# A layer of a graph network on one core: destinations' rows from a table in memory, 28 of 48 copied columns on VectorE, a ring of twenty groups

## The chip, the core and the metric

The kernel runs on one core of a Trainium2 chip. The core has five engines with a queue of instructions each: TensorE (PE in the profile; PEld is its loading of weights), VectorE (DVE), ScalarE (ACT), GpSimd (POOL) and SyncE (SP, which issues DMAs). An engine's queue is worked off in order by its sequencer; the profile writes what the sequencer does itself, such as loading registers, with a q behind the engine's name (DVEq), and does not count it as busy time. The metric is the time on the device, in microseconds.

## What is computed

One message-passing layer with a residual and a layer norm. There are 12500 nodes with 64 features and 212500 edges, sorted by destination, with 32 features each.

```python
msg_in = jnp.concatenate([nodes[row], nodes[col], edge_features], axis=-1)
messages = relu(msg_in @ mW1 + mb1) @ mW2 + mb2
aggregated = jax.ops.segment_sum(messages, col, num_segments=nodes.shape[0])
upd_in = jnp.concatenate([nodes, aggregated], axis=-1)
x = layernorm(nodes + relu(upd_in @ uW1 + ub1) @ uW2 + ub2)
```

`row` is the source of an edge and `col` its destination. All is in 32-bit floating point.

## The kernel before

The edges are cut into 554 groups of 384, a group into three tiles of 128 edges. Since the edges are sorted by destination, the destinations of one group lie in a window of 32 consecutive nodes, whose first node is known from the list `firsts`. One step of the main loop (`for k in range(G)`, line 560) works on several groups at once, each in a different stage:

- `gather` (line 146): GpSimd fetches the source nodes' 64 features of a group, one indirect DMA for each tile of 128 rows, into a ring of buffers `own_s`. The ring has `RING = AHEAD + 4 = 8` groups. A gather that fills a buffer anew waits for the transpose of the group that had it before.
- `onehot` (line 326): VectorE compares each edge's destination with the 32 positions of the window and writes a matrix of zeros and ones beside the gathered features.
- `turn(k)` (line 335): TensorE transposes the three tiles, features and one-hot columns together; ScalarE copies the result into `own_st`, where the edges' own features already lie.
- `hidden(k - 2)` (line 361): TensorE multiplies `own_st` by the matrix `own_wm` of the group. Its first 64 rows are the source's part of `mW1`, its last 32 the edge's part; the 32 rows in the middle hold, for each node of the window, that node's features times the destination's part of `mW1` (the window's rows). There are `NW = 8` such matrices, used in turn. ScalarE then applies the relu (`own_h`).
- `sums(k - 4)` (line 387): TensorE sums the hidden rows by destination with the one-hot matrix and counts the edges; VectorE adds both to `agg` and to a row of `own_xc`, at the window's place (lines 406 and 407).

The window's rows come about in two parts. `places` (line 296), every fourth step, loads the first nodes of four windows into VectorE's registers and copies the four windows out of `own_xc`, the transposed features of all nodes, which lie in SBUF. `windows` (line 311) multiplies the four by the destination's part of `mW1` in one product on TensorE; VectorE copies the result into four of the matrices `own_wm` (line 320).

Not every tile is gathered. The first tile of some groups is put together column by column: `fetch` (line 475) loads the addresses of some source nodes into registers (line 490) and copies one column of `own_xc` into `own_st` for each edge (lines 503 and 505). From step `BEGIN = 18` to step 543 there are 40 columns a step: VectorE takes batches of 8 and 12, ScalarE batches of 12 and 8. Each batch is one register load of as many registers, and then as many copies of 64 partitions by 4 bytes. The groups so served are listed in `COPIED`. The addresses come by SyncE's queue for eight steps at a time (`indexes`), and VectorE turns them into byte addresses (`addresses`).

Twenty-five blocks of 512 nodes are finished as soon as no later edge can reach them (`update`, line 413), one part a step: the second products, the statistics, the normalisation, and the output by SyncE's queue. The last `SHORT = 10` groups go through the stages one after the other, so that the end is short.

The order of work is the order in which the program writes it, engine by engine (`manual_schedule`). In one step VectorE's queue holds the two additions, in every fourth step the four copies of line 320, the comparison, then a register load, 8 columns, a register load, 12 columns, and in every fourth step the load and copies of `places`. `step` (line 524) puts all of a step's products behind one wait, and what follows them waits for the last product of the step.

Of the kernel before, what the change touches and what calls it, by code (L numbers as in the profile page):

```python
# [10 lines left out]
F32 = mybir.dt.float32  # L11
# [23 lines left out]
AHEAD = 4  # L35
# [9 lines left out]
NEAR_GROUPS = 24  # L45
# [4 lines left out]
VCOLS = (8, 12)  # L50
# [29 lines left out]
PLAN = plan()  # L80
COPIED = []
# [27 lines left out]
def ordered(ctx: ExitStack, tc: tile.TileContext, a, own, ok):  # L109
# [6 lines left out]
    xwp = ctx.enter_context(tc.tile_pool(name="xw", bufs=2))  # L116
# [29 lines left out]
    def gather(g):  # L146
# [9 lines left out]
        for i in loads[g]:  # L156
            after(i, *([turn_by[g // 2 * 2 + 1 - RING]] if g >= RING else []))
# [55 lines left out]
    nc.vector.memset(high[:, :NEAR_GROUPS], float(NEAR_NODES - W))  # L213
# [33 lines left out]
    starts, xws, indices, columns_by = {}, {}, {}, {}  # L247
# [48 lines left out]
    def places(b):  # L296
# [8 lines left out]
        xw = xwp.tile([D + 2, SB, W], F32, name="xw")  # L305
        for i in range(n):
            starts[g + i] = v[i]
            nc.vector.tensor_copy(xw[:, i, :], xc[:, bass.ds(v[i], W)])  # L308
        xws[b] = xw, n

    def windows(b, wp, own_bank=True):


        xw, n = xws.pop(b)
        did = nc.tensor.matmul(wp[: n * W, :], xw[:, :n, :], w1b, start=True, stop=True)  # L315

        def copies():
            for i in range(n):
                g = b * SB + i
                c = nc.vector.tensor_copy(wm[g % NW][D : D + W, :], wp[i * W : (i + 1) * W, :])  # L320
                after(c, *([did] if own_bank else []), *([hidden_by[g - NW]] if g >= NW else []))
                wm_by[g] = c

        return did, copies
# [62 lines left out]
    def sums(g, ps):  # L387
# [14 lines left out]
        def add(step):  # L402
            sums_by[g] = step
            at = bass.ds(starts.pop(g), W)
            return [
                after(nc.vector.tensor_tensor(agg[:, at], sg[:, 0, :], agg[:, at], ALU.add), step),  # L406
                after(nc.vector.tensor_tensor(xc[D : D + 1, at], counted,  # L407
                                              xc[D : D + 1, at], ALU.add), step),
            ]
# [65 lines left out]
    def fetch(k):  # L475
# [4 lines left out]
        if n == 0:  # L480
            indexes(i + 1)
        if n == SPAN - 2:
            addresses(i + 1)
        c0 = (k - BEGIN) * COLS
        for engine, count in [*((ET.DVE, c) for c in VCOLS), *((ET.Activation, c) for c in ACOLS)]:
# [21 lines left out]
            c0 += count  # L507
# [16 lines left out]
    def step(*work):  # L524
# [9 lines left out]
        copies = None  # L534
        for part, g, *_ in parts:
# [389 lines left out]
```

## Time and profile before

| | |
|---|---|
| median of 3 runs | 1899.2 us (1896.05 to 1899.49) |
| the profiled execution | 1895.48 us |
| its span, first to last instruction | 1893.5 us |
| granted TensorE clock, mean | 0.969 |
| instructions in the span | 58044 |
| gathers on GpSimd | 1497 |
| columns on VectorE, on ScalarE | 10500, 10492 |

A row of a group gives the line, the engine, the operation, what is written and read, and the count; behind the bar the busy time in us and the mean of one in ns; behind the second bar the idle time of the engine just before, and what ended most of it. "issue" means that the engine waited for nothing that the profile shows as a wait. A row of the order in time gives start and length in us, and the idle time in brackets. A row of one line's instructions gives the shortest, the median and the longest duration in ns, and the first and the last start in us.

### The profile page before, as it was taken

The numbers are of one execution on the slowest core, as the hardware profiler recorded it, in microseconds if no ns is written. First come the engines' busy times: TensorE is split into PE (matmuls) and PEld (weight loads), VectorE is DVE, ScalarE is ACT, GpSimd is POOL, SyncE is SP. The second block draws the span as 40 slices with busy tenths as digits, with TensorE's granted clock in tenths as the row PEclk, the third lists the DMA queues.
The fourth block names the chain that finished last, engine by engine and source line by source line (L and its number), as shares of the span: only waits on it lengthen the run. The fifth ranks groups of instructions, "written<-read, shape, count | busy, mean of one in ns | idle before, by whom it ended". The sixth has DMA issues, their size and how long they took to land. (4 is left out here: it accounts for less than half of the span.)

```text
span 1893.5 us, 58044 instructions
## 1 busy us (share of the span) xinstructions
PE 1361.4 (72%) x12209; PEld 1193.4 (63%) x12209; DVE 1492.9 (79%) x13761; ACT 1550.7 (82%) x11818; POOL 1417.6 (75%) x1504
## 2 busy tenths in 40 slices
PE   3776777677777777677676776877767767767777
PEld 3666666666666666666665666666666656666665
DVE  3578888778888788887888878878888887888873
ACT  3489889888888888988988888889888888898882
POOL 7777777777777777777777777777777777777774
PEclk9999999999999999999999999999999999999999
DMA  6322222222222222222222222222222222222221
GB/s 136 73 46 45 46 48 44 50 43 48 46 45 48 47 43 50 45 46 44 48 50 43 48 46 45 46 48 44 50 44 47 47 48 44 47 44 50 44 47 29
DMA packets 68440, 92.50 MB, mean 49 GB/s; under 512 B 30893, under 2 KB 38350, under 8 KB 68078
## 3 DMA queue, kind: packets, MB, share of 16 engines
q0 software_dynamic: 47904, 49.12, 14.7%
q1 hardware_dynamic: 19260, 39.12, 7.4%
q14 instruction: 260, 2.13, 0.4%
q8 instruction: 102, 1.67, 0.4%
q10 hardware_dynamic: 914, 0.46, 0.1%
HBM read 85.29 MB, written 3.20 MB: 47 GB/s over the span
## 5 line engine op out<-in xcount | busy, mean ns | idle before, releaser
L149 POOL DMA_INDIRECT own_s<-in_x,src_sb x1497 | 1416.8, 946 | 457.3 <-issue 407.5
L503 DVE COPY own_st<-own_xc 64x4 uint8 x10500 | 897.7, 190 | 231.0 <-issue 217.9
L505 ACT ACTIVATE own_st<-own_xc 64x4 uint8 x10492 | 1057.1, 194 | 18.2 <-issue 15.2
L341 PE MATMUL own_ps<-own_ident,own_s 128*96 128x128 f32 x1661 | 289.5, 285 | 496.0 <-DMA own_s<-in_x,src_sb 157.9
L341 PEld LDWEIGHTS own_ps<-own_ident,own_s 128*96 128x96 f32 x1661 | 169.3, 132 | 566.1 <-ACT own_h L377 240.7
L394 PE MATMUL own_ps<-own_s,own_h 128*128 128x128 f32 x3322 | 480.5, 283 | 4.1 <-ACT own_h L377 2.9
L366 PE MATMUL own_ps<-own_wm,own_st 128*128 128x128 f32 x3322 | 479.4, 283 | 0.0
L351 ACT ACTIVATE own_st<-own_ps 96x384 f32<-96x384 f32 (+2 forms) x718 | 293.2, 408 | 205.8 <-PE own_ps L399 104.7
L394 PEld LDWEIGHTS own_ps<-own_s,own_h 128*128 128x128 f32 x3322 | 432.6, 199 | 6.3 <-ACT own_h L377 4.7
L366 PEld LDWEIGHTS own_ps<-own_wm,own_st 128*128 128x128 f32 x3322 | 432.1, 199 | 1.4 <-issue 0.5
L377 ACT ACTIVATE own_h<-own_ps 128x384 f32<-128x384 f32 x553 | 263.9, 477 | 16.0 <-PE own_ps L366 16.0
L399 PE MATMUL own_ps<-own_s,own_one 128*1 128x32 f32 x3322 | 190.1, 194 | 0.0
L320 DVE COPY own_wm<-own_ps 32x128 f32<-32x128 f32 x550 | 156.9, 285 | 5.6
L399 PEld LDWEIGHTS own_ps<-own_s,own_one 128*1 128x1 f32 x3322 | 114.5, 84 | 69.4 <-issue 6.2
L329 DVE TENSOR_TENSOR own_s<-iota,dlc 128x96 f32<-128x96 f32 x554 | 142.4, 258 | 14.3 <-issue 0.2
L406 DVE TENSOR_TENSOR agg<-own_ps,agg 128x32 f32 x554 | 105.1, 190 | 59.5 <-PE own_ps L399 25.9
L407 DVE TENSOR_TENSOR own_xc<-own_ps,own_xc 1x32 f32 x554 | 101.2, 183 | 30.6 <-PE u_ps L425 11.4
L308 DVE COPY xw<-own_xc 66x32 f32 x554 | 73.0, 207 | 15.5 <-DMA own_xc<-in_xT 9.8
L315 PE MATMUL own_ps<-w1b,xw 66*128 66x128 f32 (+1 forms) x276 | 69.1, 333 | 0.0
L446 ACT ACTIVATE rstd<-mv,eps 128x4 f32<-128x4 f32 (+1 forms) x25 | 7.4, 297 | 55.3 <-DVE mv L444 55.3
L437 PE MATMUL u_ps<-u,u 128*128 128x64 f32 (+1 forms) x196 | 50.1, 399 | 0.5 <-ACT u L427 0.5
L437 PEld LDWEIGHTS u_ps<-u,u 128*128 128x128 f32 (+1 forms) x196 | 47.1, 324 | 2.2 <-ACT u L427 0.9
(62 smaller groups left out, 276.7 us busy)
## 6 DMA issues: line engine op xcount, KB each, us to landing
own_st<-in_efT SPq DMA_DIRECT2D x138, 192.0 KB
own_s<-in_x,src_sb POOLq DMA_INDIRECT x1497
xin<-in_x SPq DMA_DIRECT2D x24, 128.0 KB
out<-o SPq DMA_DIRECT2D x24, 128.0 KB
own_xc<-in_xT SPq DMA_DIRECT2D x12, 179.2 KB
index<-in_src_copied SPq DMA_DIRECT2D x65, 1.2 KB
dlc_i<-in_dst_cols SPq DMA_DIRECT2D x1, 831.0 KB
own_xc<-in_xT SPq DMA_DIRECT2D x4, 179.5 KB
```

What stands on the lines that cost most here:

```text
L149: nc.gpsimd.indirect_dma_start(out=s[:p, j, :D], out_offset=None, in_=x[:, :], in_offset=bass.IndirectOffsetOnAxis(ap=src_sb[:p, g * TG + ...
L320: c = nc.vector.tensor_copy(wm[g % NW][D : D + W, :], wp[i * W : (i + 1) * W, :])
L329: places_by[g] = nc.vector.tensor_tensor(own.s[g % RING][:, :, D:], iota.unsqueeze(1).to_broadcast([P, TG, W]), dlc[:, g * TG : (g + 1) * ...
L341: nc.tensor.transpose(xt[:, j * P : j * P + p], s[:p, j, :], ident[:p, :p])
L351: after(nc.scalar.activation(t[r, c : c + n][:, m], xt[r, m], AF.Copy), step)
L366: nc.tensor.matmul(pre[:p, j, :], t[:, c + j * P : c + j * P + p], wm[g % NW], start=True, stop=True)
L377: relu_by[g] = [nc.scalar.activation(h, pre, AF.Relu)]
L394: did.append(nc.tensor.matmul(sg, h[:p, j, :], s[:p, j, D:].unsqueeze(1).to_broadcast([p, TIMES, W]), start=j == 0, stop=j == len(sizes) - 1))
L399: did.append(nc.tensor.matmul(counted, own.one[:p], s[:p, j, D:], start=j == 0, stop=j == len(sizes) - 1))
L406: after(nc.vector.tensor_tensor(agg[:, at], sg[:, 0, :], agg[:, at], ALU.add), step),
L503: by[engine] = nc.vector.tensor_copy(o, x_at)
L505: by[engine] = nc.scalar.activation(o, x_at, AF.Copy)
```

## The change

Three things change together.

The ring of gathered groups grows from 8 to 20 buffers (`AHEAD` from 4 to 16), and a gather now waits for the transpose of exactly the group that had its buffer.

The window's rows are no longer worked out window by window. A table of all nodes' products with the destination's part of `mW1` is written to memory in 25 blocks of up to 512 nodes: two before the loop, the others in every third step (`projected`: four small products on TensorE, a copy on ScalarE, a DMA by SyncE's queue). For each group SyncE reads 32 rows of the table straight into the matrix `own_wm` (`window`), four steps ahead of the group's transpose; the first node is loaded into SyncE's registers for four groups at a time. VectorE's copies of lines 308 and 320 and TensorE's product of line 315 are gone; VectorE still loads the first nodes for its own additions. Limits on the windows' places (`LIMITS`) see to it that no row is read before its block is written.

Columns grow from 40 to 48 a step: on VectorE batches of 12, 8 and 8, on ScalarE 12 and 8 as before. The three batches on VectorE are no longer together: the first stands between the two additions, the second after them, the third after the comparison.

```diff
-AHEAD = 4
+AHEAD = 16
 RING = AHEAD + 4
-NEAR_GROUPS = 24
+EVERY = 3
+LIMITS = (0, 24, 48)
-VCOLS = (8, 12)
+VCOLS = (12, 8, 8)
 ACOLS = (12, 8)
...
-            after(i, *([turn_by[g // 2 * 2 + 1 - RING]] if g >= RING else []))
+            after(i, *([turn_by[g - RING]] if g >= RING else []))
...
         for i in range(n):
             starts[g + i] = v[i]
-            nc.vector.tensor_copy(xw[:, i, :], xc[:, bass.ds(v[i], W)])
-        xws[b] = xw, n
-
-    def windows(b, wp, own_bank=True):
...
+    def projected(c):
+        base, n = TABLE[c]
+        ps = ups.tile([H, CH], F32, name="u_ps").rearrange("p (n h) -> p n h", n=4)
+        for j in range(n):
+            nc.tensor.matmul(ps[:, j], xc[:, base + j : base + n * P : n], w1b,
+                             start=True, stop=True)
+        t = rowp.tile([P, 4, H], F32, name="t")
+        nc.scalar.activation(t[:, :n], ps[:, :n], AF.Copy)
+        written.append(after(nc.sync.dma_start(
+            by_dst[base : base + n * P, :].rearrange("(p n) h -> p n h", n=n), t[:, :n])))
+
+    def window(g):
...
+        if g % SB == 0:
+            n = min(SB, G - g)
+            _, v = nc.values_load_multi_w_load_instructions(
+                start_i[0:1, g : g + n], engines=[ET.SP], min_val=0, max_val=N - 1,
...
+        wm_by[g] = nc.sync.dma_start(wm[g % NW][D : D + W, :],
+                                     by_dst[bass.ds(rows_at.pop(g), W), :])
+        after(wm_by[g], *written, *([hidden_by[g - NW]] if g >= NW else []))
+        written.clear()
...
-            return [
-                after(nc.vector.tensor_tensor(agg[:, at], sg[:, 0, :], agg[:, at], ALU.add), step),
-                after(nc.vector.tensor_tensor(xc[D : D + 1, at], counted,
-                                              xc[D : D + 1, at], ALU.add), step),
-            ]
+            a = after(nc.vector.tensor_tensor(agg[:, at], sg[:, 0, :], agg[:, at], ALU.add), step)
+            if between:
+                between.pop()()
+            return [a, after(nc.vector.tensor_tensor(xc[D : D + 1, at], counted,
+                                                     xc[D : D + 1, at], ALU.add), step)]
...
-    windows(0, ups.tile([H, CH], F32, name="u_ps")[:, :H], False)[1]()
+    projected(0)
+    projected(1)
+    for g in range(SB):
+        window(g)
...
+        if k % EVERY == 0 and 0 < k // EVERY < len(TABLE) - 1:
+            projected(k // EVERY + 1)
...
         if k < G - SHORT:
+            between.append(lambda: fetch(k, 0))
             step((turn, k), *([(hidden, k - 2)] if k > 1 else []),
                  *([(sums, k - 4)] if k > 3 else []))
             made, summed = max(0, k - 1), max(0, k - 3)
+            if between:
+                between.pop()()
+            fetch(k, 1)
...
+        window(k + SB)
         onehot(k + 2)
-        fetch(k)
+        if k < G - SHORT:
+            fetch(k, *range(2, len(VCOLS + ACOLS)))
```

`fetch(k, *parts)` now emits the batches named by `parts`; the loading of the next addresses and their arithmetic moved to the end of the step.

54 lines of the change are left out of this document (24 added, 30 removed).

## The prediction

> **What bounds the kernel now.** I read the page's busy times first, then the gathers' rows early and late, then VectorE's own order in time, because the change moves work from GpSimd to VectorE.
>
> ```profile
> PE 1361.4 (72%) x12209; PEld 1193.4 (63%) x12209; DVE 1492.9 (79%) x13761; ACT 1550.7 (82%) x11818; POOL 1417.6 (75%) x1504
> L149 POOL DMA_INDIRECT own_s<-in_x,src_sb x1497 | 1416.8, 946 | 457.3 <-issue 407.5
> ```
>
> ScalarE shows the largest share, but GpSimd is the bound: its 1497 gathers take 1416.8 us and the 457.3 us before them are fixed gaps of 0.3 us. The longest wait tells that:
>
> ```profile
> POOL own_s L149 <- issue: 407.5, 1337, 0.3
> L149 POOL DMA_INDIRECT own_s<-in_x,src_sb x59 | 57.1, 968 | 19.1 <-issue 17.1 <-DMA src_sb<-in_src 1.4 <-DMA own_s<-in_x,src_sb 0.3
> L149 POOL DMA_INDIRECT own_s<-in_x,src_sb x1411 | 1334.1, 946 | 430.0 <-issue 383.7 <-DMA own_s<-in_x,src_sb 35.1 <-PE own_ps L399 10.1
> L149 POOL DMA_INDIRECT own_s<-in_x,src_sb x1497: 901/944/1612, 2.9 to 1874.8; - x188
> ```
>
> The second row is the window from 4 to 78 us, before any column is copied, the third from 82 to 1845 us. (1334.1 + 430.0)/1411 = 1.250 us a gather, without a break from 2.9 to 1874.8 us. A step (a group of 384 edges) has 3 - 40/128 = 2.6875 gathers, so 3.36 us; that times 526 steps is the middle of the kernel. The last gather starts 18.7 us before the end of the span of 1893.5 us.
>
> The other limit is close. VectorE's rows, a stretch of its order in time, then its register loads in two windows that hold one load each (eight registers, then twelve; the ScalarE rows are left out):
>
> ```profile
> 80.24 0.19 DVE L406 TENSOR_TENSOR agg<-own_ps,agg 128x32 f32 x1 [4.26 <-PE own_ps L399]
> 80.46 0.18 DVE L407 TENSOR_TENSOR own_xc<-own_ps,own_xc 1x32 f32 x1
> 80.68 0.26 DVE L329 TENSOR_TENSOR own_s<-iota,dlc 128x96 f32<-128x96 f32 x1
> 81.15 0.66 DVE L503 COPY own_st<-own_xc 64x4 uint8 x8 [0.22 <-ACT own_h L377]
> 82.32 0.96 DVE L503 COPY own_st<-own_xc 64x4 uint8 x12 [0.51 <-issue]
> 83.20 0.17 DVE L406 TENSOR_TENSOR agg<-own_ps,agg 128x32 f32 x1
> 83.40 0.18 DVE L407 TENSOR_TENSOR own_xc<-own_ps,own_xc 1x32 f32 x1
> 83.62 0.26 DVE L329 TENSOR_TENSOR own_s<-iota,dlc 128x96 f32<-128x96 f32 x1
> 83.79 0.73 DVE L503 COPY own_st<-own_xc 64x4 uint8 x8
> 84.96 0.95 DVE L503 COPY own_st<-own_xc 64x4 uint8 x12 [0.43 <-issue]
> ```
> ```profile
> L490 DVEq TENSOR_LOAD <-index x1: 594/594/594, 1006.8 to 1006.8; - x1
> L490 DVEq TENSOR_LOAD <-index x1: 844/844/844, 1007.7 to 1007.7; - x1
> L490 DVEq TENSOR_LOAD <-index x1050: 591/843/1118, 80.5 to 1844.6; - x175
> L301 DVEq TENSOR_LOAD <-start_i x139: 340/344/594, 13.8 to 1863.6; - x139
> ```
>
> Before each batch of columns VectorE's queue loads the batch's addresses into registers. The loads don't count as busy, yet the queue does nothing else meanwhile: four registers take 344 ns, eight 594, twelve 844, which is 62.5 ns a register and some 94 ns a load, whatever the engine does. From the first column of a batch of eight to the first of the batch of twelve pass 82.32 - 81.15 = 1.17 us, and 84.96 - 83.79 = 1.17 again: the load's 0.844 and eight columns at 0.04 us of the queue. From 82.32 to 83.79, 1.47 us, it is twelve columns (0.49), the load of eight (0.594), and 0.39 for the two sums, the comparison and their address arithmetic. So one step needs 1.17 + 1.47 = 2.64 us of VectorE's queue, though its columns occupy the engine only (0.95 - 0.66)/4 = 0.072 us each (a batch of twelve against one of eight). Where VectorE catches up with GpSimd, the queue's 2.64 us is its pace, not the engine's.
>
> **The change, part by part.**
>
> Gathers: 1497 become 1465 (48 columns a step make a 128-row tile every 2.67 steps). That is 32 x 1.250 = 40 us less on GpSimd, and 2.625 x 1.250 = 3.28 us a step.
>
> Columns on VectorE: batches 8, 12 become 12, 8, 8, the first between the two sums, the second after them, the third after the comparison. The queue's work by the numbers above: loads 0.844 + 2 x 0.594 = 2.03, columns 28 x 0.04 = 1.14, the rest 0.39, together 3.56 us against 2.64. The instructions beside which the loads now stand are cover for the engine, not for the queue, which has no slack of its own left: 3.56 is over 3.28.
>
> Windows: VectorE loses two copies a step; beside them the rows of what else its queue has:
>
> ```profile
> L320 DVE COPY own_wm<-own_ps 32x128 f32<-32x128 f32 x524 | 149.5, 285 | 5.3
> L308 DVE COPY xw<-own_xc 66x32 f32 x524 | 69.2, 207 | 2.3 <-issue 2.3
> L473 DVE TENSOR_SCALAR index<-index 1x320 int32<-1x320 int32 x64 | 24.0, 374 | 0.0
> L439 DVE TENSOR_TENSOR y<-u_ps,xin 128x256 f32<-128x256 f32 x23 | 9.8, 424 | 18.3 <-PE u_ps L437 18.2
> L443 DVE BATCH_NORM_STATS2 stats<-y 128x6 f32<-128x64 f32 x92 | 18.6, 202 | 0.8
> L444 DVE BATCH_NORM_AGGREGATE mv<-stats 128x2 f32<-128x6 f32 x92 | 16.7, 182 | 3.1
> L454 DVE TENSOR_SCALAR o<-y,mv,rstd 128x64 f32<-128x64 f32 x92 | 23.7, 333 | 0.9
> ```
>
> The two copies are 218.7 us of engine time, 0.42 us a step. In the new kernel that is worth nothing by itself, since the engine (28 x 0.072 + 0.59 from 83.20 to 83.79 = 2.61 us a step) is not what is full; the 2.64 us above held no window. What a step adds beside the 3.56: the load of four starts every fourth step (0.344/4 = 0.09), the index arithmetic every eighth (0.374/8 = 0.05), and one chunk's update every 22 steps (0.42 + 4 x 0.202 + 4 x 0.182 + 4 x 0.333 = 3.3 us, 0.15 a step). The update is engine time and runs partly under the queue's loads: between 0 and 0.15, I take 0.05. Sum: 3.75 us a step, between 3.56 (all three hidden) and 3.85; with the present waits of VectorE for TensorE and ScalarE kept in full, some 0.1 more, 3.95.
>
> SyncE gets 554 window reads and 25 table writes in its queue, and loads of four addresses every fourth step.
>
> ```profile
> L195 SPq DMA_DIRECT2D own_wm<-in_mW x8: 317/582/583, 13.6 to 22.9; - x8
> SPq L289 <- PE own_ps L399: 1113.2, 119, 14.4
> SPq L458 <- DVE own_xc L407: 293.6, 24, 21.8
> ```
>
> A DMA of the window's shape takes SyncE 0.3 to 0.58 us, so under 0.8 us a step with the loads; the queue now waits over 1400 us. A window for group k+4 is sent in step k, after the hidden product of group k-4, and is read in step k+6. Behind it stand only loads two blocks ahead. An output that waits for VectorE holds later windows by a step at most. I cost this at nothing in the middle; the cover is those six steps, over 20 us.
>
> TensorE loses 274 window products and gains 98 small ones, ScalarE gains 25 copies of a bank in the first 72 steps; both wait for others already (ScalarE's 1550.7 us over 554 steps is 2.8 us). Cost nothing.
>
> The ring of 20 groups lets GpSimd run ahead of a slow VectorE. It saves no time where VectorE is the bound.
>
> The start: the first hidden product now waits for the table's first rows.
>
> ```profile
> 13.19 10.66 ACT L243 ACTIVATE agg<-zero 128x12544 f32<-128x12544 f32 x1
> 27.19 1.40 PEld L366 LDWEIGHTS own_ps<-own_wm,own_st 128*128 128x128 f32 x6
> ```
>
> ScalarE is free at 23.9 us, then come two copies, a DMA out and a DMA in. [...]
>
> The end: after step 543 no columns are copied; from 1846 us to the end of the span are 47 us, of which the groups' serial chain (hidden product, relu, sums) is the most and GpSimd little. I take 46.
>
> The sum: 86 + 526 x 3.75 (1972.5) + 46 = 2104.5 us of span, and 2 us around it as in the profiled execution (1895.5 against a span of 1893.5): 2106 us. The median of the runs, 1899.2, lies 0.2% over the profiled execution, and a difference under 0.2% is about what a measurement of this kernel can't tell from no change.
>
> **Rivals.**
>
> 1. The loads are hidden, and GpSimd stays the bound. Then VectorE needs 2.61 us of engine and 0.2 us of updates and index work a step, under 3.28, and the kernel gains the 40 us: 1855. For it: the page puts only 217.9 us of idle on the 1050 loads. Against it: the quickest steps go at the queue's sum. It decides where VectorE's mean step falls below 3.35 us, (1895.5 - 134)/526, that is if 0.4 us of the 3.75 goes under other work (134 as in rival 2).
>
> ```profile
> L503 DVE COPY own_st<-own_xc 64x4 uint8 x10500 | 897.7, 190 | 231.0 <-issue 217.9
> ```
>
> [...]
>
> 2. Each load stalls the engine as now, 217.9 us/1050 = 0.21 us, and no more. Then a step is 2.61 + 3 x 0.21 + 0.2 = 3.44 us and the time 526 x 3.44 + 134 = 1943 (134 is the 86, 46 and 2 of the sum). Against it: the present stall is small because the batch of eight is loaded beside three other operations; with queue and engine nearly in step each load has less to hide under.
>
> 3. The windows come late: TensorE waits for a read behind a waiting output on SyncE's queue. From the product of group g-8, which frees a window's buffer, to that of group g are eight steps, so it decides from 8 x 3.75 = 30 us on. SyncE's two longest waits one behind the other (14.4 and 21.8 us in the rows above) in every round would make it 36.2/8 = 4.5 us a step, 526 x 4.5 + 134 = 2501. Against it: the waits for outputs come 24 times in the whole kernel.
>
> **How the numbers follow.** The queue on VectorE as the bound: 0.79, its own range 2006 (3.56) to 2180 (3.89; the waits of 3.95 in full would be 2212). Rival 2, or a part of the loads hidden: 0.11, 1900 to 2006. Rival 1: 0.08. Rival 3: 0.02. The range from 1950 to 2185 leaves out rivals 1 and 3 and the ends of the others, under 2 in 10. Faster 0.08, same 0.01, slower 0.91.
>
> **What would show it.** Right: VectorE's sums of two successive steps lie 3.5 us apart or more; idle before the columns, put on issue, grows to hundreds of us; GpSimd now waits for TensorE's transposes (its ring is full) and its gathers' gaps exceed 0.3 us; three loads a step of 844, 594, 594 ns; SyncE's window reads land well before use. Wrong: gathers still follow at 1.25 us, or loads that take less, or columns that start during a load.

## The result and the profile after

| | before | after |
|---|---|---|
| median of 4 runs | 1898.1 us | 2262.3 us (2260.3 to 2267.8) |
| ratio, 95% interval | | 1.192 (1.190 to 1.195) |
| the profiled execution, its span | 1895.5, 1893.5 us | 2262.3, 2260.5 us |
| granted TensorE clock, mean | 0.969 | 0.893 |

The direction is the one predicted; the time is 156 us over the predicted 2106 us and 77 us over the end of the range.

The page of the changed kernel, its busy times, the clock by fortieths of the span, and three of its groups:

```profile
PE 1478.4 (65%) x12127; PEld 1309.2 (58%) x12127; DVE 1613.1 (71%) x16799; ACT 1579.4 (70%) x11827; POOL 1384.9 (61%) x1472
...
PEclk9787878899999999899899898898998989999988
...
L153 POOL DMA_INDIRECT own_s<-in_x,src_sb x1465 | 1384.1, 945 | 794.4 <-PE own_ps L416 413.5
L518 DVE COPY own_st<-own_xc 64x4 uint8 x14644 | 1277.9, 185 | 434.5 <-issue 317.1
...
L320 PE MATMUL u_ps<-w1b,own_xc 66*128 66x128 f32 x196 | 53.8, 447 | 104.6 <-DVE own_xc L425 77.6
```

No engine is busy for more than 71% of the span. GpSimd, which TensorE hardly kept waiting before, now idles 794.4 us, more than half of it for TensorE's last product of a step. So its ring is full and something behind it sets the pace. The idle time that VectorE's columns have from "issue", which is where the register loads lie, went from 217.9 to 317.1 us.

VectorE's order in time in the middle of the kernel, one plain step (VectorE's waits are in brackets), and the register loads of the whole kernel:

```profile
999.87 0.17 DVE L422 TENSOR_TENSOR agg<-own_ps,agg 128x32 f32 x1
1000.69 1.12 DVE L518 COPY own_st<-own_xc 64x4 uint8 x12 [0.65 <-issue]
1001.84 0.18 DVE L425 TENSOR_TENSOR own_xc<-own_ps,own_xc 1x32 f32 x1
1002.06 0.66 DVE L518 COPY own_st<-own_xc 64x4 uint8 x8
1002.63 0.24 DVE L346 TENSOR_TENSOR own_s<-iota,dlc 128x96 f32<-128x96 f32 x1
1002.85 0.67 DVE L518 COPY own_st<-own_xc 64x4 uint8 x8
1003.44 0.17 DVE L422 TENSOR_TENSOR agg<-own_ps,agg 128x32 f32 x1
```
```profile
L505 DVEq TENSOR_LOAD <-index x1569: 591/596/866, 98.0 to 2207.3; - x197
```

From sum to sum pass 1003.44 - 999.87 = 3.57 us. The engine is idle for only 0.65 us of them, in front of the batch of twelve; the other two loads stand beside columns that the engine still has to finish. Yet the pace is that of the queue: 3.56 was the prediction's sum of loads, columns and the rest. Measured in the queue, from the start of one load of twelve to the next, the median over the some 284 plain steps from 90 to 530 (no load of four, no index arithmetic, no update) is 3.560 us. From sum to sum the same steps have a median of 3.65 us. All times of plain, statistics and output steps below are from load to load; means over many steps are from sum to sum. Here and below a step bears the number of the group whose sums are added in it, so step 14 is the first one with columns.

Where the time lies, told by two places: the first additions of a step with columns, and the same additions 526 steps later (VectorE's order in time):

```profile
98.03 0.19 DVE L422 TENSOR_TENSOR agg<-own_ps,agg 128x32 f32 x1 [5.03 <-PE own_ps L416]
```
```profile
2213.55 0.19 DVE L422 TENSOR_TENSOR agg<-own_ps,agg 128x32 f32 x1 [0.71 <-PE own_ps L416]
```

| part | predicted | measured | difference |
|---|---|---|---|
| up to the first column batch | 86 | 98.0 | +12 |
| 526 steps at the steady pace | 526 x 3.75 = 1972.5 | 526 x 3.900 = 2051.4 | +79 |
| slower steps at the beginning | 0 | 2115.5 - 2051.4 | +64 |
| the end | 46 | 2260.5 - 2213.55 = 47.0 | +1 |

(2115.5 is 2213.55 - 98.03; 3.900 is the mean from step 134 to step 530.) The four differences are the 156 us. The third row needs a look at the early stage, in which the table is still being written. By twenties from step 14 on the mean step is 5.25, 5.49 and 4.68 us, then 3.77 and 3.90. The three slow twenties lose 74 us, of which some 10 come back: 3 us in the twenty behind them, 8 us in the last ten steps with columns, at 3.12 us each. TensorE and VectorE in this stage (order in time, each engine's waits in brackets):

```profile
149.21 0.34 PE L416 MATMUL own_ps<-own_s,own_one 128*1 128x32 f32 x6
154.49 2.21 PE L320 MATMUL u_ps<-w1b,own_xc 66*128 66x128 f32 x8 [4.95 <-DVE own_xc L425]
156.49 0.85 PE L358 MATMUL own_ps<-own_ident,own_s 128*96 128x128 f32 x3
157.13 1.49 PE L383 MATMUL own_ps<-own_wm,own_st 128*128 128x128 f32 x6
...
162.41 0.83 PE L383 MATMUL own_ps<-own_wm,own_st 128*128 128x128 f32 x6
```
```profile
151.85 0.19 DVE L422 TENSOR_TENSOR agg<-own_ps,agg 128x32 f32 x1
153.16 0.97 DVE L518 COPY own_st<-own_xc 64x4 uint8 x12 [1.12 <-ACT own_st L520]
154.16 0.18 DVE L425 TENSOR_TENSOR own_xc<-own_ps,own_xc 1x32 f32 x1
...
161.42 0.19 DVE L422 TENSOR_TENSOR agg<-own_ps,agg 128x32 f32 x1 [5.13 <-PE u_ps L441]
```

The table's products (line 320) read `own_xc` with all its 66 rows, and one of these rows is the count to which VectorE adds at line 425. The program writes the products behind the additions of the step before, so TensorE has to wait for line 425. TensorE has finished that step's products at 149.55. VectorE, still at the columns of the step before, comes to the first addition only at 151.85, and the second one now stands behind a register load and twelve columns besides: TensorE is idle for 4.95 us, until VectorE has done it at 154.34. Then it is VectorE that waits, 5.13 us, for the step that TensorE begins late. And TensorE is slow behind its pause: six hidden products take 1.49 us instead of 0.83. Windows of the trace show the clock (length; busy time and count of PE, PEld, DVE, ACT, POOL; granted clock, DMA share, GB/s). First the pause and what follows it, then the stage in which the table is written and the rest, all after; last, before, a stretch of the same length from the first columns on:

```profile
149.60:153.40 3.80, 0.00 (x0) 0.00 (x0) 2.33 (x29) 3.21 (x27) 2.83 (x4) 1.00 0.15 28
153.50:160.30 6.80, 5.81 (x30) 5.48 (x30) 2.67 (x28) 0.60 (x1) 5.13 (x6) 0.50 0.35 94
98.00:300.00 202.00, 130.49 (x918) 118.47 (x918) 114.64 (x1202) 117.69 (x869) 124.45 (x133) 0.79 0.22 53
300.00:2208.00 1908.00, 1245.68 (x10474) 1101.20 (x10475) 1457.88 (x15415) 1417.60 (x10885) 1187.51 (x1258) 0.91 0.20 44
```
```profile
81.00:284.00 203.00, 147.85 (x1333) 129.55 (x1332) 161.81 (x1532) 173.45 (x1333) 153.63 (x163) 0.97 0.22 46
```

In 202 us the changed kernel executes 1202 instructions on VectorE where the old one executed 1532, at a granted clock of 0.79 against 0.97. The clock falls while TensorE still stands idle (0.99 from 153.0 to 153.5 us, 0.50 from 153.5 to 154.4, and TensorE starts at 154.49), after the pause the same six products take 1.49/0.83 = 1.8 times as long, and those that start at 162.41 are back at 0.83. In front of the table's products TensorE makes eleven such pauses, of 4.20 to 6.84 us, between 103 and 268 us; the clock is 1.00 in the 2 us ahead of each and 0.50 in the second us behind it. In this stage the clock falls without such a pause too, as the run "Without the row" below shows.

One thing is needed to read the numbers of some experiments: in two sittings the kernel before itself took a third longer (2551.5 and 2559.4 us), and a trace taken there puts hundreds of microseconds on a releaser that the profile doesn't know ("remote"), as in this row from the waits of a kernel with the same loads, columns and products as before; runs of those sittings (called disturbed below) are compared only with each other.

```profile
ACT own_st L351 <- remote: 367.0, 117, 7.7
```

### The profile page after: what moved, and what is told of

Its sections match the earlier page's. It is cut to its first block, busy times and chain, and to the rows that moved or that the text cites. A ratio compares the mean times of both kernels' runs of the same rounds, so it can differ in the third digit from the quotient of the medians.

```text
span 2260.5 us, 63792 instructions
## 1 busy us (share of the span) xinstructions
PE 1478.4 (65%) x12127; PEld 1309.2 (58%) x12127; DVE 1613.1 (71%) x16799; ACT 1579.4 (70%) x11827; POOL 1384.9 (61%) x1472
## 3 DMA queue, kind: packets, MB, share of 16 engines
q8 instruction: 102, 1.67, 0.3%
## 5 line engine op out<-in xcount | busy, mean ns | idle before, releaser
L153 POOL DMA_INDIRECT own_s<-in_x,src_sb x1465 | 1384.1, 945 | 794.4 <-PE own_ps L416 413.5
L518 DVE COPY own_st<-own_xc 64x4 uint8 x14644 | 1277.9, 185 | 434.5 <-issue 317.1
L358 PE MATMUL own_ps<-own_ident,own_s 128*96 128x128 f32 x1661 | 315.3, 304 | 659.7 <-ACT own_h L394 417.9
L411 PE MATMUL own_ps<-own_s,own_h 128*128 128x128 f32 x3322 | 530.9, 303 | 4.2 <-ACT own_h L394 3.6
L383 PE MATMUL own_ps<-own_wm,own_st 128*128 128x128 f32 x3322 | 522.7, 299 | 0.0
L411 PEld LDWEIGHTS own_ps<-own_s,own_h 128*128 128x128 f32 x3322 | 483.1, 219 | 6.4 <-ACT own_h L394 5.2
L383 PEld LDWEIGHTS own_ps<-own_wm,own_st 128*128 128x128 f32 x3322 | 474.8, 215 | 2.2 <-issue 0.5
L320 PE MATMUL u_ps<-w1b,own_xc 66*128 66x128 f32 x196 | 53.8, 447 | 104.6 <-DVE own_xc L425 77.6
L320 PEld LDWEIGHTS u_ps<-w1b,own_xc 66*128 66x128 f32 x196 | 47.5, 327 | 108.3 <-issue 95.6
L323 ACT ACTIVATE t<-u_ps 128x512 f32<-128x512 f32 (+1 forms) x25 | 14.7, 588 | 73.8 <-PE u_ps L320 70.8
```

The source lines that it names most:

```text
L153: nc.gpsimd.indirect_dma_start(out=s[:p, j, :D], out_offset=None, in_=x[:, :], in_offset=bass.IndirectOffsetOnAxis(ap=src_sb[:p, g * TG + ...
L320: nc.tensor.matmul(ps[:, j], xc[:, base + j : base + n * P : n], w1b, start=True, stop=True)
L358: nc.tensor.transpose(xt[:, j * P : j * P + p], s[:p, j, :], ident[:p, :p])
L383: nc.tensor.matmul(pre[:p, j, :], t[:, c + j * P : c + j * P + p], wm[g % NW], start=True, stop=True)
L411: did.append(nc.tensor.matmul(sg, h[:p, j, :], s[:p, j, D:].unsqueeze(1).to_broadcast([p, TIMES, W]), start=j == 0, stop=j == len(sizes) - 1))
L518: by[engine] = nc.vector.tensor_copy(o, x_at)
```

## The experiments

The theory: VectorE's queue sets the pace, through the register loads (0.094 us a load and 0.0625 us a register); besides, the table's products wait for VectorE's addition in the first 74 steps. The rivals: the copies themselves or the table cost the time, the gathers do, or each load costs a fixed stall.

### What the loads are worth

**No loads on VectorE.** The 28 columns are still copied, but from places known when the program is written, so VectorE loads no registers for them.

```diff
-            _, v = nc.values_load_multi_w_load_instructions(
+            if engine == ET.DVE:
+                v = [None] * count
+            else:
+                _, v = nc.values_load_multi_w_load_instructions(
...
-                x_at = xc_bytes[:D, bass.ds(at - own.at, 4)]
+                x_at = (xc_bytes[:D, 4 * c : 4 * c + 4] if at is None
+                        else xc_bytes[:D, bass.ds(at - own.at, 4)])
```

> The changed kernel, but VectorE's 28 columns are copied from fixed places, without register loads (so the copied source features are not the edges' own). If VectorE's queue with its loads is the bound, its step falls from 3.56 us to the engine's 2.6 and the gathers' 3.28 us are the bound: about 1870 us (1855 to 1900). If the copies themselves, the window reads or the chain of products are the bound, it stays above 2150 us.

Measured: 1865.2 us (before 1898.3). Its groups:

```profile
L153 POOL DMA_INDIRECT own_s<-in_x,src_sb x1465 | 1386.0, 946 | 456.4 <-issue 298.3 <-DMA own_s<-in_x,src_sb 109.4 <-PE own_ps L416 43.4
...
L522 DVE COPY own_st<-own_xc 64x4 uint8<-64x4 uint8 x14644 | 1249.8, 186 | 15.7
```

The same 14644 copies of the same 186 ns, without their loads, are 397 us faster, and the gathers are the bound again, (1386.0 + 456.4)/1465 = 1.258 us each. The loads are the price, and neither the engine's part of the copies nor the order of the batches. With the loads the copies' register addresses are gone too; what those cost in the queue this run doesn't separate, but the five loads of four below vary the loads alone. The slow beginning is still there, if shorter (4.27, 4.45 and 3.76 us a step by twenties from step 14), but it costs little in the end: afterwards the steps go at 2.96 to 2.99 us, faster than the gathers' 3.28, until the groups that GpSimd has gathered ahead are used up.

**The change without its eight more columns.**

```diff
-VCOLS = (12, 8, 8)
+VCOLS = (12, 8)
```

> Table and ring as changed, but VectorE's columns back to 20 a step in batches of 12 and 8 (spread as changed). If VectorE's queue is the bound: 3.56 - 0.594 - 8 x 0.04 = 2.65 us and 0.35 of extras a step, under the gathers' 3.36, so 1895 to 1940 us, with some loss left in the first 72 steps. If the table's reads and writes are what is slow, above 2100 us.

Measured: 1922.1 us (before 1898.3). Steps 14 to 74 take 4.72, 4.99 and 4.09 us by twenties, where before they took 3.59, 3.37 and 3.34, so that 70 us are lost, and 13 more ahead of step 14 (its sum comes at 93.3 us, not 80.2). From step 134 on the mean step is 3.264 us, less than before (3.367) and than the gathers' own pace of 3.36. That fits the ring of twenty as in the run before: during the slow beginning GpSimd gathers on, and its lead is used up later, 396 x 0.10 = 41 us, about what twelve more groups of 3.36 us hold. Most of the loss comes back, not all of it. The kernel before has no such beginning with 20 columns, so it comes with the table, the ring or the order of the batches and not with the eight more columns.

**The eight more columns without the rest**, in the kernel before:

```diff
-VCOLS = (8, 12)
+VCOLS = (12, 8, 8)
```

> The kernel before with 28 columns a step on VectorE in batches of 12, 8 and 8 behind the comparison; no table, ring of 8. If VectorE's queue is the bound: 3.56 us, 0.35 of extras and 0.1 to 0.2 for the windows' copies, 81 + 526 x 4.05 + 47 = 2260 us (2200 to 2300). If the table is what is slow, 1860 to 1950 us.

Measured: 2298.9 us (before 1898.3), a mean step of 4.148 us, and no slow beginning (4.24, 4.18, 4.16).

```profile
L149 POOL DMA_INDIRECT own_s<-in_x,src_sb x1465 | 1385.6, 946 | 875.7 <-PE own_ps L399 483.8 <-issue 381.4 <-DMA own_s<-in_x,src_sb 8.5
```

Third batch and eight columns add 0.594 + 8 x 0.04 = 0.91 us of queue a step; the step grew by 4.148 - 3.367 = 0.78. So VectorE's queue had some 0.13 us of slack a step before the change, if the new load costs no more than its own time. The rest of the change, which is the table, the ring and the places of the batches, is worth 4.148 - 3.900 = 0.25 us a step. The two traces show where: from sum to sum the plain steps have the same mean in both kernels (3.68 us), but every fourth step, in which the copies of four windows stand, takes 4.80 us in this one against 3.91 (5.10 against 4.10 with index arithmetic). A quarter of 0.9 to 1.0 us is the 0.25, so it is the table that saves it. The whole change is in these two sizes: +0.78 - 0.25 = +0.53 us a step.

**Five loads of four instead of one of eight and one of twelve**, in the kernel before: the same columns, copies and gathers, and three loads more.

```diff
-VCOLS = (8, 12)
+VCOLS = (4, 4, 4, 4, 4)
```

> Five loads of four instead of 8 and 12, the columns unchanged, on a chip on which the kernel before takes its usual 1898 us. Queue as the bound: 3.55 us a step, 1995 us (1940 to 2040). If only copies and waits count, 1898 us.

Measured: 2088.1 us (before 1896.8). Loads and gathers, then two batches in VectorE's order in time:

```profile
L490 DVEq TENSOR_LOAD <-index x2625: 335/341/539, 79.0 to 2035.5; - x188
```
```profile
L149 POOL DMA_INDIRECT own_s<-in_x,src_sb x1497 | 1414.6, 945 | 631.7 <-issue 402.3 <-PE own_ps L399 207.9 <-DMA own_s<-in_x,src_sb 19.5
```
```profile
1002.14 0.38 DVE L503 COPY own_st<-own_xc 64x4 uint8 x4
1002.68 0.38 DVE L503 COPY own_st<-own_xc 64x4 uint8 x4 [0.16 <-issue]
```

Nothing but the split of the loads differs, and it costs 191 us. The load is thus paid for by itself in VectorE's queue, as the theory has it. It is more than the expected 1995 us and lies over the end of its range, 2040: the batches follow 0.54 us apart, where 0.341 and four columns at 0.04 make 0.50; the step grew by 3.731 - 3.367 = 0.36 us, of which 5 x 0.341 - 0.594 - 0.844 = 0.27 is the loads' own time. The remaining 0.09, or 0.03 for each load more, wasn't taken apart; the 60 to 80 ns that some expectations put around a load are shown by no row. The same edit in a disturbed sitting:

> The kernel before with VectorE's 20 columns a step in five batches of four instead of 8 and 12: the same columns, copies and gathers, three register loads more a step. Queue as the bound: the loads take 5 x 0.344 = 1.72 us instead of 1.44 and some 0.07 around each of the three, 2.64 + 0.49 and 0.4 of extras is about 3.55 us a step against the gathers' 3.36: 1995 us (1940 to 2040). If only copies and waits count, 1898 us.

It took 2611.3 us against 2559.4 there, and tells little, since something else limits both in that sitting.

**One load more in front of each step's columns**, in the kernel before (eight registers that nothing uses):

```diff
+        b = c0 - i * SPAN * COLS
+        if c0 + 8 <= P * len(COPIED):
+            nc.values_load_multi_w_load_instructions(
+                indices[i][0:1, b : b + 8], engines=[ET.DVE],
...
```

> The kernel before with one more register load of eight addresses a step on VectorE, and nothing copied by them. If the queue is the bound, a load costs 0.594 us and some 0.08 around it: 2.64 + 0.67 and about 0.45 of extras (with the windows' copies) is 3.76 us a step against the gathers' 3.36, so 81 + 526 x 3.76 + 47 = 2106 us (2040 to 2150). If only the engine's work counts, a load is free and the time stays at 1898 us.

> The kernel before with one more register load of eight addresses a step on VectorE, nothing copied by them; on a chip on which the kernel before takes its usual time. Queue as the bound: about 3.76 us a step, 2106 us (2040 to 2150). Engine's work alone: 1898 us.

Measured: 2569.0 us (before 2551.5), and in an undisturbed sitting 1897.6 (before 1896.9). The experiment is void, as the row of its loads shows: there are 1050, as before. The added loads, whose registers nobody reads, aren't in the program that ran.

```profile
L497 DVEq TENSOR_LOAD <-index x1050: 593/834/1103, 79.5 to 1844.1; - x175
```

### The slow beginning

**The table's products ahead of the additions.** Only their place in the program's order differs: each is written behind the step's own products and ahead of its additions, so that it waits for the additions of the step before, which are done by then.

```diff
             if part is sums:
+                if due:
+                    projected(due.pop())
                 step_update(g)
...
-            projected(k // EVERY + 1)
+            due.append(k // EVERY + 1)
+            if k < 4:
+                projected(due.pop())
```

> The changed kernel with the table's products ahead of the step's additions, on such a chip. If the wait behind twelve columns makes the first 72 steps slow, steps 14 to 74 take about 4.1 us instead of 5.1 and the time is 2180 to 2210 us. If not, 2262 us.

Measured: 2197.9 us (before 1896.9): 64 us less than the changed kernel. TensorE's group of these products, in the window from 98 to 300 us, after and then in this experiment; and this kernel's first sum of a step with columns:

```profile
L320 PE MATMUL u_ps<-w1b,own_xc 66*128 66x128 f32 x96 | 26.5, 455 | 56.0 <-DVE own_xc L425 53.0 <-ACT own_st L520 3.1
```
```profile
L320 PE MATMUL u_ps<-w1b,own_xc 66*128 66x128 f32 x132 | 34.6, 410 | 11.0 <-DVE own_xc L425 11.0
```
```profile
87.42 0.19 DVE L422 TENSOR_TENSOR agg<-own_ps,agg 128x32 f32 x1 [1.38 <-PE own_ps L416]
```

In the same stretch the wait for line 425 falls from 53.0 to 11.0 us while more of the products are done; the columns start at 87.4 us instead of 98.0, near the predicted 86; steps 14 to 74 take 4.32, 4.20 and 3.97 us. The steady step is the same (3.913 us, plain steps 3.558). So the place of the products, and with it the wait for line 425, caused most of the late start and of the slow beginning, and nothing of the steady pace. Some 15 us of a slow beginning remain. The same kernel in a disturbed sitting:

> The changed kernel with the table's products put ahead of the step's additions in the program, so that they wait for the additions of the step before, which are long done. If the wait behind twelve columns is the cause of the slow start, the time is as without the wait: 2180 to 2210 us. If not, 2262 us.

It took 2451.4 us (before 2551.5). Its steps 14 to 74 took 4.77, 4.55 and 4.26 us, with 4.26 later on, some 16 us lost in the beginning.

**Without the row.** To take the dependency away altogether, the products read only the 64 feature rows, and the bias comes by a second product with a row of ones.

```diff
-            nc.tensor.matmul(ps[:, j], xc[:, base + j : base + n * P : n], w1b,
-                             start=True, stop=True)
+            nc.tensor.matmul(ps[:, j], xc[:D, base + j : base + n * P : n], w1b[:D],
+                             start=True, stop=False)
+            nc.tensor.matmul(ps[:, j], ones[0:1, :], b1, start=False, stop=True)
```

> The changed kernel, but the table's products read only the 64 rows of features (the bias comes by a second product with a row of ones), so that they need not wait for VectorE's addition to the row of counts in the same buffer. If that wait is what makes the first 72 steps slow, steps 14 to 54 go from 5.4 us to about 3.95 and the time falls by 70 to 90 us, to 2170 to 2195. If not, it stays at 2262 us.

Measured: 2261.2 us (before 1898.3), no gain. The products in the window from 100 to 300 us:

```profile
L322 PE MATMUL u_ps<-w1b,own_xc 64*128 64x128 f32 x109 | 41.4, 464 | 0.8 <-ACT u L447 0.8
L324 PE MATMUL u_ps<-b,ones 1*128 1x128 f32 x108 | 31.3, 376 | 0.0
```

The wait in front of them is gone (0.8 us instead of 56.0). But the second product is nearly as dear as the first, the sum of step 14 comes only at 119.7 us, and steps 14 to 74 still take 4.66, 4.97 and 4.26 us. The run removes a wait and adds work at the same place: TensorE is now busy for 192.5 of the 202 us from 98 to 300 (130.5 in the changed kernel), so that it sets the pace of this stage by its work instead of its pauses.

And its clock is as low without the pauses, 0.77 in that window. In the round at 150 us TensorE works without a break (windows of this run's trace, columns as above), and still the clock falls to half in the midst of the table's products:

```profile
150.90:155.70 4.80, 4.80 (x31) 4.01 (x32) 3.69 (x40) 4.78 (x41) 3.58 (x5) 1.00 0.26 67
155.80:162.50 6.70, 6.70 (x31) 5.65 (x32) 3.06 (x32) 1.74 (x8) 5.17 (x6) 0.50 0.25 72
```

So a pause isn't needed for the half clock; what in these products brings it about no run shows. Taken alone this run doesn't decide on the cause of the slow beginning in the changed kernel; in its own, TensorE's work bounds this stage.

**Without the row and without the bias** in the table, in a disturbed sitting:

```diff
-            nc.tensor.matmul(ps[:, j], xc[:, base + j : base + n * P : n], w1b,
+            nc.tensor.matmul(ps[:, j], xc[:D, base + j : base + n * P : n], w1b[:D],
```

> The changed kernel with the table's products over the 64 feature rows alone, one product a tile as changed (the bias of the first layer is left out of the table). They don't wait for VectorE's addition to the counts, and TensorE gets no more work. If that wait makes the first 72 steps slow, steps 14 to 74 fall from 5.1 us to 4.0 and the time to 2180 to 2200 us. If the half clock of TensorE there has another cause, the steps stay above 4.6 us and the time above 2240 us.

Measured: 2442.8 us (before 2551.5). Steps 14 to 74 take 4.55, 4.42 and 4.38 us against 4.25 later on: about 12 us lost in the beginning, as little as in the reordered kernel of the same sitting (16 us). The changed kernel itself wasn't run in that sitting, and there every step is slowed by something else, so this points to the wait and shows it no more than that.

### Fewer and longer loads

**Two batches of fourteen**, in the changed kernel; one load fewer for the same columns.

```diff
-VCOLS = (12, 8, 8)
+VCOLS = (14, 14)
```

> The changed kernel with VectorE's 28 columns in two batches of 14. If a load's own part (94 ns, and some 80 around it) is paid by the queue, the step falls by 0.15 to 0.2 us, 80 to 105 us in all: 2155 to 2185 us. If only the registers and columns count, 2262 us.

Measured: 3569.6 us, in a sitting where before took 2551.5, far outside what was expected. The loads themselves are the reason (shortest, median, longest in ns):

```profile
L505 DVEq TENSOR_LOAD <-index x1046: 1309/2253/3196, 173.1 to 3507.8; - x175
```

Fourteen registers take 1.31 us in the first load of a step and 3.2 us in the second. On VectorE batches of 4, 8, 12 and 16 took 0.341, 0.594, 0.844 and 1.09 us, which is 62.5 ns a register and 94 ns a load. The addresses lie one behind the other; each of those batches begins a whole number of fours behind the list's start and is itself of whole fours, while the second batch of fourteen begins fourteen addresses behind the first. So the prediction's price was met for whole fours at such places and for nothing else that was run. An estimate from the measured times: in the first load the two registers beyond twelve cost (1.309 - 0.844)/2 = 0.23 us each, in the second all fourteen cost (3.18 - 0.094)/14 = 0.22 us each. What makes a register so dear, the number or the place, wasn't shown: neither was varied alone.

**Sixteen and twelve**, which keeps whole fours:

```diff
-VCOLS = (12, 8, 8)
+VCOLS = (16, 12)
```

> VectorE's 28 columns in batches of 16 and 12, so two register loads instead of three, each of a multiple of four registers. If a load costs 94 ns and 62.5 ns a register (1.09 us for sixteen), and some 60 ns around it, the step falls from 3.90 us to 3.72 to 3.77, the time to 2165 to 2195 us. If a load of more than twelve registers is slow by itself, as two of fourteen were (1.3 and 3.2 us), the step rises over 4.2 us.

```profile
L505 DVEq TENSOR_LOAD <-index x1046: 842/974/1112, 95.5 to 2181.5; - x175
```

Measured: 2239.3 us (before 1896.9), 23 us less than the changed kernel and well over what was expected. The loads take what the theory says (0.84 and 1.09 us), and the plain step has a median of 3.40 us against 3.56, as expected. But the mean of the plain steps falls by only 0.10 us (3.66 to 3.56), and steps with a chunk's statistics take about 6.6 us instead of about 5.8, so that the mean over all falls by 0.06 us. A load saved in the plain step is partly given back in the others; why the update costs more with two batches is open.

### A version that beats both

From these runs follows a version: VectorE keeps 20 columns, the four more go to ScalarE, whose waits were long, and the table's products stand ahead of the additions. The edits are `VCOLS = (12, 8)`, `ACOLS = (12, 12)` and the reordering above, all in the changed kernel.

> Table with its products ahead of the additions, ring of 20, 20 columns a step on VectorE (12 and 8) and 24 on ScalarE (12 and 12). VectorE's queue needs 3.0 us a step, the gathers 2.656 x 1.25 = 3.32, ScalarE 0.96 + 24 x 0.1 = 3.36: at best 1880, more likely 1890 to 1915 us. If the register loads on ScalarE cost as on VectorE, above 1950 us.

> Table with its products ahead of the additions, ring of 20, 20 columns on VectorE and 24 on ScalarE, on such a chip: 1876 us, a ratio of 0.988 to 0.99 to the kernel before.

Measured: 1875.9 us in a first run, a little under the best that was expected, then 1874.8 (1873.8 to 1876.7, 4 runs) against 1896.8 for before, a ratio of 0.9888 (0.9872 to 0.9905). That is a small gain, 1.1%, but one outside the spread of the runs. The page's rows, then ScalarE's columns and register loads:

```profile
PE 1374.2 (73%) x12127; PEld 1210.5 (65%) x12127; DVE 1267.0 (68%) x12635; ACT 1718.4 (92%) x13927; POOL 1401.8 (75%) x1488
...
L153 POOL DMA_INDIRECT own_s<-in_x,src_sb x1481 | 1401.0, 946 | 452.5 <-issue 352.7 <-DMA own_s<-in_x,src_sb 81.4 <-PE own_ps L416 13.4
...
L520 ACT ACTIVATE own_st<-own_xc 64x4 uint8 x12560 | 1254.7, 200 | 17.0 <-issue 15.8 <-DVE own_st L518 0.7
...
L505 ACTq TENSOR_LOAD <-index x1047: 547/782/1088, 89.9 to 1819.7; - x175
```

The gathers are the bound again, 16 fewer than before. ScalarE's loads of twelve take nearly what VectorE's do (0.78 against 0.84 us), yet its columns wait on "issue" for only 15.8 us in all, not for hundreds: a column keeps ScalarE for 1254.7/12560 = 0.10 us, so a batch of twelve is 1.2 us of engine work, more than the load behind it. The expectation's condition, that loads on ScalarE cost as on VectorE, was thus met by their length and not by their effect. ScalarE stands at 92%, so there is little more to give it.

Which part of it gains, the ring, the table or ScalarE's columns, was asked in a disturbed sitting: this version again, the same with the ring of 8, and the kernel before with the ring of 20 and 24 columns on ScalarE but no table.

> Table with its products ahead of the additions, ring of 20, 20 columns on VectorE and 24 on ScalarE, in five rounds: 1876 us as in the single run, faster than before by 1.1%.

> The same with the ring of 8 groups. If the deep ring helps where steps differ (GpSimd would otherwise stop in the slow first steps), the time is 15 to 40 us more; if GpSimd never waits, 1876 us.

> The kernel before with a ring of 20 and 24 columns on ScalarE (12 and 12), without the table. VectorE's queue needs 2.64 and 0.45 of extras and windows, 3.1 us, under the gathers' 3.32: 1878 to 1890 us if the table is not needed at 20 columns; above 1900 us if VectorE's windows now bind.

They took 2427.7, 2405.0 and 2417.8 us against 2559.4 for before, with ratios of 0.949 (0.946 to 0.952), 0.941 (0.937 to 0.945) and 0.945 (0.941 to 0.949). There all three gain some 5 to 6%, and neither the larger ring nor the table shows an advantage. How the 1.1% of the undisturbed sitting divides among the parts is open.

## Why the prediction was right and where it was wrong

**Right: the bound and the plain step.** VectorE's queue sets the steady pace. Loads of 844, 594 and 594 ns, 28 columns at 0.04 us and 0.39 for the rest were to make 3.56 us; the median plain step is 3.560. All that was to show it is in the trace: the sums lie 3.5 us or more apart, idle on "issue" grows, and GpSimd waits for TensorE. The run without loads and the five loads of four show that it is the loads.

**Wrong, 76 us: "TensorE loses 274 window products and gains 98 small ones ... Cost nothing", and the start at 86 us.** The count compares two different things. A row counts two instructions for each of these products, as the 3322 hidden ones of 1661 tiles show; TensorE loses 276 such instructions (before, below) and gains 196, that is 138 products against 98, and the new ones are dearer, 447 against 333 ns an instruction.

```profile
L315 PE MATMUL own_ps<-w1b,xw 66*128 66x128 f32 (+1 forms) x276 | 69.1, 333 | 0.0
```

The count doesn't matter much, though: the new products wait. The step looked at what TensorE has to do and not at what the new products read, although a row of `own_xc` is written by the addition at line 425, and the change itself puts a load and twelve columns in front of that addition. It cost 12 us at the start against the sum's 86, and, net of what came back, 64 in the steps behind it. The reordering alone took 64 of these 76 us away. What the 86 us allow for the way of the table's first rows to memory and back no run shows by itself; measured, SyncE sends the first rows from 24.09 us on, TensorE's wait for the first window ends at 31.72, the first hidden product begins with its load of weights at 32.15 (27.19 before), and the first column batch comes at 98.0, or at 87.4 with the products ahead of the additions. Neither this nor the next step alone carries the result out of the range: 2106 + 76 = 2182 us lies just inside, and with 526 steps of 3.900 and the predicted start and end it would have been 86 + 2051.4 + 46 + 2 = 2185 us, the range's upper end. Both together do.

**Mis-sized, 79 us: what a step adds beside the 3.56.** Predicted 0.19 us a step, measured 3.900 - 3.560 = 0.34:

| term | predicted | measured | how |
|---|---|---|---|
| load of four, every fourth step | 0.09 | 0.11 | such steps have a mean of 4.10 us, plain ones 3.66 |
| index arithmetic, every eighth | 0.05 | 0.02 | 0.13 us more than a step with a load of four alone |
| update, every 22nd step | 0.05 | 0.12 | step with the statistics 5.76, with the outputs 4.16, against 3.66 |
| not foreseen | 0 | 0.10 | mean of plain steps 3.66 against a median of 3.56 |

The update was taken as lying partly under the loads. Most of it doesn't: from the first of its operations to the end of the last statistics pass 1024.33 - 1022.45 = 1.9 us of the engine, and such a step is 2.1 us longer than a plain one (VectorE's order in time after):

```profile
1022.45 0.42 DVE L456 TENSOR_TENSOR y<-u_ps,xin 128x256 f32<-128x256 f32 x1 [0.18 <-PE u_ps L454]
...
1024.15 0.18 DVE L461 BATCH_NORM_AGGREGATE mv<-stats 128x2 f32<-128x6 f32 x1
```

The prediction's upper bound for the step, 3.85 or 3.95 with the waits, held 3.90; the middle was chosen too low in it.

**The window copies, "worth nothing by itself".** Wrong as put: against the kernel before with 28 columns the table saves 0.25 us a step, all of it in the steps with the copies. It didn't enter the sum, since the 3.56 us held no window. That run also shows that VectorE's queue, and not only GpSimd, was close to the bound before: with one load more the step grew at once by nearly its whole price.

**Costed at nothing, and rightly: SyncE's queue and the windows.** One wait of the changed kernel is put on a window, that of the start (its waits: total, times, longest), so rival 3 fails. The larger ring bought the changed kernel nothing, since it was full: GpSimd waited 413.5 us for buffers.

```profile
POOL own_s L153 <- PE own_ps L416: 413.5, 256, 7.0
...
PE own_ps L358 <- DMA own_wm<-by_dst: 4.1, 1, 4.1
```

**The rivals.** Rival 1 (loads hidden, 1855 us) fails on the run without loads, which lands at 1865.2: that is the kernel which rival 1 describes, and the changed one is 397 us slower. The columns behind a load take their addresses from its registers, and the rows show them waiting for its end: before, the batch at 82.32 us has 0.51 us of idle in front of it, and in the kernel with five loads of four the second batch starts 0.54 us after the first though the engine is idle for 0.16 us in front of it. Whether instructions that need none of the registers go ahead during a load, no run varied. Rival 2 (a fixed 0.21 us for each load, 1943 us) fails on the plain step of 3.56 us where it has 3.44 with all extras.

## What to carry to other kernels

A register load was time of VectorE's queue here, 2.03 of the 3.56 us of a plain step, and did not show as the engine's busy time: add up what the queue does in one step, loads included, and compare that sum with the other engines' pace before work is moved there. ScalarE's loads of twelve in the last version, 0.78 us in the median, were hidden behind its own queued work, 1.2 us of columns a batch: 15.8 us of idle for 1047 loads. For each new instruction ask what it reads and who writes next to it in the same buffer, down to the single row, and what now stands ahead of that writer in its queue; here, behind eleven such waits of 4.20 to 6.84 us, one every third step, TensorE's clock stood at 0.50 as well. Terms that come every fourth or every 22nd step belong in the sum with their whole length unless a row shows what hides them.

## What the runs showed of the hardware that was not expected

**Hiccups in VectorE's queue.** Of the plain steps of 3.56 us, more than a quarter (28%, from load to load) take about 0.35 us longer. Two steps of the changed kernel, in VectorE's order in time; first an ordinary one, then one with a hiccup:

```profile
519.17 0.94 DVE L518 COPY own_st<-own_xc 64x4 uint8 x12 [0.64 <-issue]
...
520.38 0.73 DVE L518 COPY own_st<-own_xc 64x4 uint8 x8
...
526.71 1.00 DVE L518 COPY own_st<-own_xc 64x4 uint8 x12 [0.77 <-issue]
...
528.27 0.69 DVE L518 COPY own_st<-own_xc 64x4 uint8 x8 [0.35 <-issue]
```

The second batch starts 1.21 us after the first in the one and 1.56 in the other. Behind the loads of twelve and the first loads of eight there are 104 such places, mostly 114 to 138 instructions of VectorE's queue apart or a multiple of that. The page's queues q14 and q8 show instruction fetches of 2.50 MB in 305 packets, 8.2 KB each, and of 1.67 MB in 102 packets. Over the 63792 instructions that is some 65 bytes for one (an estimate from the page), so 8.2 KB are about 125 instructions. That a hiccup is the fetch of the next packet of instructions is the author's estimate from these numbers; no run varied it, and the page doesn't say which engine a packet was for.

**The price of a register load by its shape.** On VectorE four registers took 0.341 us, eight 0.594, twelve 0.844, sixteen 1.09, and fourteen 1.31 in the first load of a step and 3.2 us in the second.
